# A two-layer graph network on one core: load order, place of a weight set-up, the last output, and how norms get their reciprocal root

## The chip, the core and the metric

The kernel runs on one core of a Trainium2 chip. A core has a matrix engine (TensorE, PE), a vector engine (VectorE, DVE), an activation engine (ScalarE, ACT), a general engine (GpSimd, POOL) and a queue engine (SyncE, SP). Each works through its own instructions in order, and they wait for each other by semaphores. The metric is device time in microseconds (us) for one execution; lower is better. Times given are medians over runs, and the profile shows one execution of the program.

## The reference

128 graphs of 128 nodes with 256 features go through two layers. Layer 0 is an attention layer with 8 heads, whose values depend on the kind of edge; layer 1 is a graph attention applied twice. Each layer ends in two layer norms with a feed-forward network between them. Cut to what matters:

```python
def layer0(src, adj):                      # Wq, Wk, Wv[r], Wo, W1, W2, g1, beta1, ...
    q, k = heads(src @ Wq + bq), heads(src @ Wk + bk)
    attn = softmax(q @ k.T / sqrt(32))
    out = sum((attn * (adj == r)) @ heads(src @ Wv[r] + bv[r]) for r in range(4))
    x = ln(src + merge(out) @ Wo + bo, g1, beta1)
    return ln(x + gelu(x @ W1 + b1) @ W2 + b2, g2, beta2)

def gat(h, adj, W, a):
    Wh = h @ W
    e = leaky_relu(Wh @ a[:256] + (Wh @ a[256:]).T, 0.2)
    return softmax(where(adj > 0, e, -9e15), axis=1) @ Wh

def layer1(x, adj):
    h = ln(x + gat(gat(x, adj, W1, a1), adj, W2, a2), g_ln1, b_ln1)
    return ln(h + relu(h @ w_ff1 + b_ff1) @ w_ff2 + b_ff2, g_ln2, b_ln2)

def ln(x, g, b):
    return (x - mean(x)) / sqrt(var(x) + 1e-5) * g + b
```

## The kernel before

The fast pass handles the graphs in 32 groups of G = 4 (512 tokens, T). A slower general pass follows, which a flag computed at the end switches on only for inputs that the fast pass can't treat; with these inputs it does not run. All arithmetic is in 32-bit floats.

**A group's way.** `layer0` makes `qT` and `kT` (L382, L386) and the values `v` of the four graphs (L392, L396), then for each of two pairs of graphs `scores` (L319, with Exp on ACT, L326, and the masked copy `pm` on DVE, L327) and `attended` (row sums `pden` at L342, products `pav` at L352, reciprocal and scaling on DVE), then the product with Wo (`pwo`, L412). `norm0` normalises, `x1T` transposes on PE, `first_ffn` is the network with Gelu, `layer1` holds the norm, the folded graph attention (`pw`, `pb`, `py`, `pg`) and its edge weights (`edges`, with a second use of Exp at L427). `norm2`, `x3T`, `second_ffn` (with Relu) and `written` end the group.

**What overlaps.** PE's order is written out by hand (`manual_schedule`), and the order on the other engines is found by the framework's scheduler. While PE runs `first_ffn` of group g, the units of `layer0` of group g+1 are put between its matmuls (`beside`); beside `second_ffn` of group g-1 go the units of `layer1` of group g. The first group's `layer0` runs alone ahead of the loop. The network's inner tiles `ph` and `po`, like `pq`, `pv`, `pwo` and the set-up's tiles, come from one PSUM pool, `ps_mm`, with two buffers (tag `mm`). ACT empties each `ph` into `hT` (L284), and PE can start the next but one only then.

**Norms.** `normed` (L231) takes statistics on DVE for each graph (L237, L238), adds EPS on DVE (L240), raises to the power -0.5 on GpSimd (L241, with the constant tile `mhalf`) and scales on DVE (L243). `scaled` multiplies and adds the norm's weights on GpSimd (L250, L251). There are four norms per group.

**The start.** Loads are issued from SP (`w`, `load`) and from ACT (`col`, `row`) in program order: Wq, Wk, then xT, adj and x of the first group, Wv, Wo, the networks' weights, and last the two graph weights and their vectors a1, a2, into a temporary tile that shares a buffer with `hT`. The set-up of the graph layer (L191 to L219) makes products of weights and vectors on DVE (`columns`, L89), transposes the first graph weight on PE (`pgt`), multiplies it by the second (`pgw`) and copies the results to `wu` and `wb`. It comes ahead of the first group's matmuls in PE's order. A check of each adj (L373) runs on DVE as the group is entered.

**The end.** `written` (L497) normalises a group, scales it on GpSimd, and writes all four graphs with one DMA of 512 KB.

Of the kernel before, what the change touches and what calls it, by code (L numbers as in the profile page):

```python
# [10 lines left out]
F32 = mybir.dt.float32  # L11
I32 = mybir.dt.int32
AF = mybir.ActivationFunctionType
ALU = mybir.AluOpType
# [3 lines left out]
EPS = 1e-5  # L18
# [6 lines left out]
P = 128  # L25
G = 4
T = G * P
# [3 lines left out]
class Weights:  # L31
# [40 lines left out]
    def constants(self):  # L72
        nc = self.nc
        self.ident = self.tile([P, P], "ident")
        make_identity(nc, self.ident)
        self.ones = self.tile([P, P // 4], "ones")
        nc.vector.memset(self.ones, 1.0)
        self.eps = self.tile([P, 1], "eps")
        nc.vector.memset(self.eps, EPS)
        self.mhalf = self.tile([P, G], "mhalf")  # L80
        nc.vector.memset(self.mhalf, -0.5)

    def columns(self, wt, arow, scr, name):

# [15 lines left out]
def flat(t):  # L100
    return t.rearrange("p b d -> p (b d)")


def fast_pass(ctx, tc, a, out):
# [13 lines left out]
    NF = FF // P  # L118
# [10 lines left out]
    ps_mm = ctx.enter_context(tc.tile_pool(name="ps_mm", bufs=2, space=PSUM))  # L129
    k = Weights(tc, const, a)  # L130

    def load(g):
        xt = io.tile([P, NCH, T], F32, tag="xT", name=f"xT_{g}")
        nc.sync.dma_start(
            xt, xT[:, g * T : (g + 1) * T].rearrange("(c p) t -> p c t", p=P)
        )
        ad = w3p.tile([P, G, P], I32, tag="adj", name=f"adj_{g}")
        nc.sync.dma_start(ad, adjT[:, g * G : (g + 1) * G, :])
        xr = io.tile([P, G, D], F32, tag="x", name=f"x_{g}")
        nc.sync.dma_start(  # L140
            xr, x[g * T : (g + 1) * T, :].rearrange("(b p) d -> p b d", p=P)
        )
        return xt, ad, xr


    k.constants()
    wq, wk = k.w("L0_gnn_Wq"), k.w("L0_gnn_Wk")
    first = dict(zip(("xt", "ad", "xr"), load(0)), g=0)
    bq, bk = k.col("L0_gnn_bq"), k.col("L0_gnn_bk")

    wv = k.tile([P, NCH, 2, D], "wv")
    for c in range(NCH):
        nc.sync.dma_start(
            wv[:, c], a["L0_gnn_Wv"][0:2, c * P : (c + 1) * P, :].rearrange("r p n -> p r n")
        )
        nc.vector.tensor_sub(wv[:, c, 1], wv[:, c, 1], wv[:, c, 0])
    bv = k.row("L0_gnn_bv", 2 * D)
    nc.vector.tensor_sub(bv[:, D:], bv[:, D:], bv[:, :D])
    wo, bo = k.w("L0_gnn_Wo"), k.row("L0_gnn_bo")
    w1, b1 = k.w("L0_gnn_W1"), k.col("L0_gnn_b1")  # L160
    w2 = k.w("L0_gnn_W2")
    g1c, be1c = k.col("L0_gnn_g1"), k.col("L0_gnn_beta1")
    g2c, be2c = k.col("L0_gnn_g2"), k.col("L0_gnn_beta2")
    g1r = k.row("L0_gnn_g1")

    be1b2 = k.row_sum("L0_gnn_beta1", "L0_gnn_b2")
    g2r, be2r = k.row("L0_gnn_g2"), k.row("L0_gnn_beta2")
    u1, c1 = k.w("L1_gnn_w_ff1"), k.col("L1_gnn_b_ff1")
    u2 = k.w("L1_gnn_w_ff2")
# [8 lines left out]


    NU = D + 3  # L180

    temp = flat(w1p.tile([P, NF, T], F32, tag="hT", name="temp"))
    taken = [0]

    def cut(*shape):
        n = math.prod(shape)
        taken[0] += n
        t = temp[:, taken[0] - n : taken[0]]
        return t.rearrange("p (c n) -> p c n", c=shape[0]) if len(shape) > 1 else t

    gw1, gw2 = (k.w("L1_gnn_W" + s, cut(NCH, D)) for s in "12")  # L191
    a1, a2 = (k.row("L1_gnn_a" + s, t=cut(2 * D)) for s in "12")
    scr = cut(D)
    wa1 = k.columns(gw1, a1, scr, "1")
    wa2 = k.columns(gw2, a2, scr, "2")
    rhs = cut(NCH, D + 2)
    nc.vector.tensor_copy(rhs[:, :, :D], gw2)
    nc.vector.tensor_copy(rhs[:, :, D : D + 1], wa2[:, :, 1:2])
    nc.vector.tensor_copy(rhs[:, :, D + 1 : D + 2], wa2[:, :, 0:1])
    gw1T = cut(NCH, D)  # L200
    for m in range(NCH):
        pt = mm_tile(f"pgt_{m}")
        for c in range(NCH):
            nc.tensor.transpose(
                pt[:, c * P : (c + 1) * P], gw1[:, c, m * P : (m + 1) * P], k.ident
            )
        nc.scalar.copy(gw1T[:, m, :], pt[:, :D])
    wu = k.tile([P, NCH, NU], "wu")
    wb = k.tile([P, NCH, P], "wb")
    for m in range(NCH):  # L210
        pu = mm_tile(f"pgw_{m}")
        for c in range(NCH):
            nc.tensor.matmul(
                pu[:, : D + 2], gw1T[:, c, m * P : (m + 1) * P], rhs[:, c, :],
                start=(c == 0), stop=(c == NCH - 1),
            )
        nc.scalar.copy(wu[:, m, : D + 2], pu[:, : D + 2])
        nc.vector.tensor_copy(wu[:, m, D + 2 :], wa1[:, m, 1:2])
        nc.vector.tensor_copy(wb[:, m, :], wa1[:, m, 0:1].to_broadcast([P, P]))  # L219

# [5 lines left out]
    c_out = k.tile([P, NG, G, 2], "c_out")  # L226
# [4 lines left out]
    def normed(t, n, mv=None):  # L231

        st = small.tile([P, G, 6], F32, tag="st", name="st_" + n)
        if mv is None:
            mv = small.tile([P, G, 2], F32, tag="mv", name="mv_" + n)
        for b in range(G):
            nc.vector.bn_stats(st[:, b, :], t[:, b, :])  # L237
            nc.vector.bn_aggr(mv[:, b, :], st[:, b, :])  # L238
        rs = small.tile([P, G], F32, tag="rs", name="rs_" + n)
        nc.vector.tensor_scalar(rs, mv[:, :, 1], EPS, None, op0=ALU.add)  # L240
        nc.gpsimd.tensor_tensor(rs, rs, k.mhalf, op=ALU.pow)  # L241
        for b in range(G):
            nc.vector.tensor_scalar(  # L243
                t[:, b, :], t[:, b, :], mv[:, b, 0:1], rs[:, b : b + 1],
                op0=ALU.subtract, op1=ALU.mult,
            )

    def scaled(y, gr, br, n):
        o = w3p.tile([P, G, D], F32, tag="res", name="res_" + n)
        nc.gpsimd.tensor_mul(o, y, over(gr))  # L250
        nc.gpsimd.tensor_add(o, o, over(br))  # L251
        return o
# [47 lines left out]
    def beside(main, side):  # L300

        for units in side:
            for _ in range(units):
                next(main, None)
        for _ in main:
            pass
# [180 lines left out]
    def norm0(S):  # L487
        n = "0_%d" % S["g"]
        normed(S["t0"], n)
        S["res0"] = scaled(S["t0"], g1r, be1b2, n)  # L490

    def norm2(S):
        n = "2_%d" % S["g"]
        normed(S["t2"], n)
        S["res2"] = scaled(S["t2"], h1r, he1c2, n)

    def written(S):  # L497

        g = S["g"]
        normed(S["t3"], f"3_{g}", c_out[:, g])  # L500
        o = scaled(S["t3"], h2r, he2r, f"3_{g}")
        nc.sync.dma_start(
            out[g * T : (g + 1) * T, :].rearrange("(b p) d -> p b d", p=P), o
        )

    def first_ffn(S):
        S["t1"] = t = w3p.tile([P, G, D], F32, tag="t", name="t1_%d" % S["g"])
        return ffn(t, S["x1T"], w1, b1, AF.Gelu, w2, S["res0"], "0_%d" % S["g"])
# [6 lines left out]


    def entered(g):
        return dict(zip(("xt", "ad", "xr"), load(g)), g=g)

    def x1T(S):  # L520
        S["x1T"] = transposed(S["t0"], g1c, be1c, "0_%d" % S["g"])

    def x3T(S):
        S["x3T"] = transposed(S["t2"], h1c, he1c, "2_%d" % S["g"])
# [9 lines left out]

    with tc.manual_schedule(engines={mybir.EngineType.PE}):
        cur, prev = first, None
        for _ in layer0(cur):
            pass
        norm0(cur)
        x1T(cur)  # L540
        for g in range(NG):
            nxt = entered(g + 1) if g + 1 < NG else None
            if prev:
                norm2(prev)
            beside(first_ffn(cur), turn(nxt, prev))

            def after():
                if nxt:
                    x1T(nxt)

            side = layer1(cur, after)
            if nxt:
                first_units = next(side)
                norm0(nxt)
                side = itertools.chain([first_units], side)
            beside(second_ffn(prev) if prev else iter(()), side)
            if prev:
                written(prev)
            prev, cur = cur, nxt
        norm2(prev)  # L560
        x3T(prev)
        for _ in second_ffn(prev):
            pass
        written(prev)


    ok = k.tile([P, 5], "ok")
# [353 lines left out]
```

## Time and profile before

| | us |
|---|---|
| median of 3 runs | 3092.86 |
| lowest, highest | 3091.51, 3094.2 |
| the profiled execution, as timed | 3091.51 |
| its span in the trace, first to last instruction | 3089.7 |
| mean granted clock of TensorE | 0.992 of full speed |

| engine | busy, us | instructions |
|---|---|---|
| PE weight load (beside PE) | 2018.5 | 18062 |
| DVE | 1571.7 | 3434 |
| ACT | 989.0 | 1733 |
| POOL | 881.5 | 488 |

Some rows of the costliest groups that the change touches: the GpSimd power (L241) has 128 instructions of 1053 ns on average; the scaling after it (L243) 893 ns with the norm's own statistics and 384 instructions; the GpSimd multiplication of `scaled` (L250) 2357 to 2395 ns. In a line of these views the engine stands ahead of the operation, and what is written stands left of the arrow; the shape is partitions x elements; "x" and a number count instructions; the time in brackets is how long the engine had been idle, and what ended that. In the chain of waits each line is start, length and what it was, in order of time. PEld is PE's weight load, which runs beside its matmuls. The ends of matmuls are modelled, so they are good to some tenths of a microsecond.

### The profile page before, as it was taken

The numbers are of one execution on the slowest core, as the hardware profiler recorded it, in microseconds if no ns is written. First come the engines' busy times: TensorE is split into PE (matmuls) and PEld (weight loads), VectorE is DVE, ScalarE is ACT, GpSimd is POOL, SyncE is SP. The second block draws the span as 40 slices with busy tenths as digits, with TensorE's granted clock in tenths as the row PEclk, the third lists the DMA queues.
The fourth block names the chain that finished last, engine by engine and source line by source line (L and its number), as shares of the span: only waits on it lengthen the run. The fifth ranks groups of instructions, "written<-read, shape, count | busy, mean of one in ns | idle before, by whom it ended". The sixth has DMA issues, their size and how long they took to land.

```text
span 3089.7 us, 42733 instructions
## 1 busy us (share of the span) xinstructions
PE 2998.7 (97%) x18062; PEld 2018.5 (65%) x18062; DVE 1571.7 (51%) x3434; ACT 989.0 (32%) x1733; POOL 881.5 (29%) x488
## 2 busy tenths in 40 slices
PE   3989999999999999999999999999999999999996
PEld 2556676666676666676666676666676666676664
DVE  3444564554554554554554554554555554554523
ACT  1223333323333323333233333233333233333331
POOL 0213322313322313322323322323323223322222
PEclk9999999999999999999999999999999999999998
DMA  4000000000000000000000000000000000000000
GB/s 152 21 12 23 18 18 25 21 18 25 18 18 22 24 18 25 18 18 21 25 18 25 18 18 21 25 18 24 18 18 21 25 18 25 18 18 8 8 7 15
DMA packets 58101, 69.80 MB, mean 23 GB/s; under 512 B 6704, under 2 KB 44720, under 8 KB 57904
## 3 DMA queue, kind: packets, MB, share of 16 engines
q1 hardware_dynamic: 51632, 64.76, 6.9%
q8 instruction: 144, 2.36, 0.3%
q10 hardware_dynamic: 6272, 2.25, 0.3%
q14 instruction: 53, 0.43, 0.0%
HBM read 50.22 MB, written 16.78 MB: 22 GB/s over the span
## 4 chain that ended last, share of the span: by engine, by line
PE 94%; issue 3%; DMA 1%; DVE 1%; POOL 1%; ACT 0%; POOLq 0%; DVEq 0%; ACTq 0%
PE po L291 29%; PE ph L280 28%; PE pq L382 7%; PE pv L392 7%; PE pw L452 4%; PE pav L352 4%; PE pwo L412 3%; PE pt L260 3%; PE ps L319 2%; PE pden L342 2%; PE py L467 2%; PE pg L482 2%; PE pb L459 2%; PE pb L471 1%; DVE t L243 0%
## 5 line engine op out<-in xcount | busy, mean ns | idle before, releaser
L241 POOL TENSOR_TENSOR rs<-rs,mhalf 128x4 f32<-128x4 f32 x128 | 134.0, 1053 | 1610.6 <-DVE rs L240 1610.6
L280 PE MATMUL ph<-yT,w_L_gnn_W 128*128 128x512 f32 x1024 | 481.9, 594 | 0.0
L291 PE MATMUL po<-w_L_gnn_W,hT 128*128 128x256 f32 x2048 | 472.1, 384 | 0.0
L291 PE MATMUL po<-w_L_gnn_w_ff,hT 128*128 128x256 f32 x2048 | 457.5, 379 | 0.0
L280 PE MATMUL ph<-yT,w_L_gnn_w_ff 128*128 128x512 f32 x1024 | 456.5, 594 | 0.0
L291 PEld LDWEIGHTS po<-w_L_gnn_w_ff,hT 128*128 128x128 f32 x2048 | 386.5, 190 | 65.3 <-issue 14.8
L291 PEld LDWEIGHTS po<-w_L_gnn_W,hT 128*128 128x128 f32 x2048 | 381.4, 190 | 62.2 <-issue 6.6
L284 ACT ACTIVATE hT<-ph,c_L_gnn_b_ff 128x512 f32<-128x512 f32 x256 | 175.4, 685 | 684.6 <-PE ph L280 684.6
L243 DVE TENSOR_SCALAR t<-t,mv,rs 128x256 f32<-128x256 f32 x384 | 319.3, 893 | 126.2 <-POOL rs L241 126.2
L280 PEld LDWEIGHTS ph<-yT,w_L_gnn_W 128*128 128x128 f32 x1024 | 195.2, 191 | 245.5 <-issue 230.8
L396 DVE TENSOR_TENSOR v<-pv,r_L_gnn_bv 128x512 f32<-128x512 f32 x128 | 88.5, 691 | 484.4 <-PE pv L392 484.4
L280 PEld LDWEIGHTS ph<-yT,w_L_gnn_w_ff 128*128 128x128 f32 x1024 | 188.2, 191 | 205.4 <-issue 186.6
L284 ACT ACTIVATE hT<-ph,c_L_gnn_b 128x512 f32<-128x512 f32 x256 | 175.9, 687 | 441.3 <-PE ph L280 440.9
L392 PE MATMUL pv<-wv,xT 128*128 128x512 f32 x512 | 240.2, 592 | 0.0
L359 DVE RECIPROCAL rd<-pden 128x512 f32<-128x512 f32 x64 | 214.3, 3349 | 20.8 <-PE pden L342 20.7
L327 DVE TENSOR_TENSOR pm<-e,adj 128x512 f32<-128x512 f32 x256 | 159.5, 685 | 114.3 <-ACT e L326 114.3
L237 DVE BATCH_NORM_STATS2 st<-t 128x6 f32<-128x256 f32 x512 | 192.5, 413 | 5.5
L437 POOL TENSOR_TENSOR gs<-gs,gr 128x512 f32<-128x512 f32 x64 | 66.5, 1039 | 426.3 <-DVE gr L436 415.0
L326 ACT ACTIVATE e<-ps 128x512 f32<-128x512 f32 x256 | 132.1, 603 | 152.0 <-PE ps L319 151.7
L250 POOL TENSOR_TENSOR res<-t,r_L_gnn_g 128x1024 f32<-128x1024 f32 x64 | 150.8, 2357 | 87.2 <-DVE t L243 87.2
L392 PEld LDWEIGHTS pv<-wv,xT 128*128 128x128 f32 x512 | 94.9, 190 | 108.1 <-issue 108.1
L250 POOL TENSOR_TENSOR res<-t,r_L_gnn_g_ln 128x1024 f32<-128x1024 f32 x64 | 153.3, 2395 | 31.4 <-DVE t L243 31.4
(101 smaller groups left out, 3633.5 us busy)
## 6 DMA issues: line engine op xcount, KB each, us to landing
xT<-in_xT_dram SPq DMA_DIRECT2D x32, 512.0 KB, 3.7
x<-in_x_dram SPq DMA_DIRECT2D x32, 512.0 KB, 3.9
out_dram<-res SPq DMA_DIRECT2D x32, 512.0 KB, 2.9
adj<-in_adjT_dram SPq DMA_DIRECT2D x32, 256.0 KB, 2.7
w_L_gnn_W<-in_L_gnn_W_dram SPq DMA_DIRECT2D x2, 1024.0 KB, 9.1
w_L_gnn_w_ff<-in_L_gnn_w_ff_dram SPq DMA_DIRECT2D x2, 1024.0 KB, 9.5
wv<-in_L_gnn_Wv_dram SPq DMA_DIRECT2D x2, 256.0 KB, 7.8
temp<-in_L_gnn_a_dram ACTq DMA_DIRECT2D x2, 256.0 KB, 7.5
```

Source lines behind the costliest of these rows:

```text
L237: nc.vector.bn_stats(st[:, b, :], t[:, b, :])
L241: nc.gpsimd.tensor_tensor(rs, rs, k.mhalf, op=ALU.pow)
L243: nc.vector.tensor_scalar(t[:, b, :], t[:, b, :], mv[:, b, 0:1], rs[:, b : b + 1], op0=ALU.subtract, op1=ALU.mult,)
L250: nc.gpsimd.tensor_mul(o, y, over(gr))
L280: nc.tensor.matmul(ph, wa[:, c, f * P : (f + 1) * P], inT[:, c, :], start=(c == 0), stop=(c == NCH - 1),)
L284: nc.scalar.activation(hT[:, f, :], ph, func, bias=ba[:, f : f + 1])
L291: nc.tensor.matmul(po[:, s * D : (s + 1) * D], hT[:, f, b * P : (b + 1) * P], wb_[:, f, :], start=(f == 0), stop=(f == NF - 1),)
L326: nc.scalar.activation(e[:, s], pss[s], AF.Exp, scale=SCALE)
L327: nc.vector.tensor_mul(pm[:, s], e[:, s], ad[:, 2 * p : 2 * p + 2, None, :].to_broadcast([P, 2, NCH, P]),)
L359: nc.vector.reciprocal(rd, pden)
L382: nc.tensor.matmul(pq, w[:, c, m * P : (m + 1) * P], xt[:, c, :], start=(c == 0), stop=(c == NCH - 1),)
L392: nc.tensor.matmul(pv, xt[:, c, b * P : (b + 1) * P], wv[:, c].rearrange("p r d -> p (r d)"), start=(c == 0), stop=(c == NCH - 1),)
```

## The change

Four edits are made together.

1. The first group's xT is loaded ahead of the weights, adj and x behind Wv; the graph weights and a1, a2 come ahead of Wo and the networks' weights. Both queues, SP's and ACT's, get the new order.
2. The set-up of the graph layer becomes a generator, `graph_weights`, in two parts. The first (products on DVE, transposes) is taken up after the first scores of the first group, the second (the product of the weights) after the scores of its second pair.
3. The last group is written by `written_by_graph`: statistics, root, scaling and output graph by graph, with the norm's weights applied on DVE and four DMAs of 128 KB.
4. `normed` takes the square root on ACT and its reciprocal on DVE, in place of the addition on DVE and the power on GpSimd. `mhalf` is gone.

```diff
-    def load(g):
+    def load_xT(g):
         xt = io.tile([P, NCH, T], F32, tag="xT", name=f"xT_{g}")
...
+        return xt
+
+    def load_rest(g):
         ad = w3p.tile([P, G, P], I32, tag="adj", name=f"adj_{g}")
...
     k.constants()
+    first = {"g": 0}
+    first["xt"] = load_xT(0)
     wq, wk = k.w("L0_gnn_Wq"), k.w("L0_gnn_Wk")
-    first = dict(zip(("xt", "ad", "xr"), load(0)), g=0)
     bq, bk = k.col("L0_gnn_bq"), k.col("L0_gnn_bk")
...
+    bv = k.row("L0_gnn_bv", 2 * D)
+    first["ad"], first["xr"] = load_rest(0)
+    for c in range(NCH):
         nc.vector.tensor_sub(wv[:, c, 1], wv[:, c, 1], wv[:, c, 0])
...
+    gw1, gw2 = (k.w("L1_gnn_W" + s, cut(NCH, D)) for s in "12")
+    a1, a2 = (k.row("L1_gnn_a" + s, t=cut(2 * D)) for s in "12")
+    wo = k.w("L0_gnn_Wo")
+    g1c, be1c = k.col("L0_gnn_g1"), k.col("L0_gnn_beta1")
     w1, b1 = k.w("L0_gnn_W1"), k.col("L0_gnn_b1")
...
+    def graph_weights():
+
+        scr = cut(D)
+        wa1 = k.columns(gw1, a1, scr, "1")
+        wa2 = k.columns(gw2, a2, scr, "2")
...
+            nc.scalar.copy(gw1T[:, m, :], pt[:, :D])
+        yield
+        for m in range(NCH):
+            pu = mm_tile(f"pgw_{m}")
...
@@ normed
-        nc.vector.tensor_scalar(rs, mv[:, :, 1], EPS, None, op0=ALU.add)
-        nc.gpsimd.tensor_tensor(rs, rs, k.mhalf, op=ALU.pow)
+        sd = small.tile([P, G], F32, tag="sd", name="sd_" + n)
+        nc.scalar.activation(sd, mv[:, :, 1], AF.Sqrt, bias=k.eps)
         rs = small.tile([P, G], F32, tag="rs", name="rs_" + n)
+        nc.vector.reciprocal(rs, sd)
...
+    def written_by_graph(S):
+
+        g, t = S["g"], S["t3"]
+        o = w3p.tile([P, G, D], F32, tag="res", name=f"res_3_{g}")
+        for b in range(G):
...
+            nc.vector.bn_stats(st, t[:, b, :])
+            nc.vector.bn_aggr(mv, st)
+            sd = small.tile([P, 1], F32, tag="sd", name="sd_" + n)
+            nc.scalar.activation(sd, mv[:, 1:2], AF.Sqrt, bias=k.eps)
+            rs = small.tile([P, 1], F32, tag="rs", name="rs_" + n)
+            nc.vector.reciprocal(rs, sd)
+            nc.vector.tensor_scalar(
+                t[:, b, :], t[:, b, :], mv[:, 0:1], rs, op0=ALU.subtract, op1=ALU.mult
+            )
+            nc.vector.tensor_mul(o[:, b, :], t[:, b, :], h2r)
+            nc.vector.tensor_add(o[:, b, :], o[:, b, :], he2r)
+            r0 = g * T + b * P
+            nc.sync.dma_start(out[r0 : r0 + P, :], o[:, b, :])
...
-        for _ in layer0(cur):
-            pass
+        steps = graph_weights()
+        for i, _ in enumerate(layer0(cur)):
+
+            if i in (8, 9):
+                next(steps, None)
...
-        written(prev)
+        written_by_graph(prev)
```

More of the change, by code (lines that the diff above doesn't have):

```diff
@@ L79, in constants @@
         nc.vector.memset(self.eps, EPS)
-        self.mhalf = self.tile([P, G], "mhalf")
-        nc.vector.memset(self.mhalf, -0.5)
     def columns(self, wt, arow, scr, name):
@@ L142, in load @@
         )
-        return xt, ad, xr
+        return ad, xr
     k.constants()
+    first = {"g": 0}
+    first["xt"] = load_xT(0)
     wq, wk = k.w("L0_gnn_Wq"), k.w("L0_gnn_Wk")
-    first = dict(zip(("xt", "ad", "xr"), load(0)), g=0)
     bq, bk = k.col("L0_gnn_bq"), k.col("L0_gnn_bk")
@@ L155, in fast_pass, with cut @@
         )
+    bv = k.row("L0_gnn_bv", 2 * D)
+    first["ad"], first["xr"] = load_rest(0)
+    for c in range(NCH):
         nc.vector.tensor_sub(wv[:, c, 1], wv[:, c, 1], wv[:, c, 0])
-    bv = k.row("L0_gnn_bv", 2 * D)
     nc.vector.tensor_sub(bv[:, D:], bv[:, D:], bv[:, :D])
-    wo, bo = k.w("L0_gnn_Wo"), k.row("L0_gnn_bo")
+    bo = k.row("L0_gnn_bo")
+    temp = flat(w1p.tile([P, NF, T], F32, tag="hT", name="temp"))
+    taken = [0]
+    def cut(*shape):
+        n = math.prod(shape)
+        taken[0] += n
+        t = temp[:, taken[0] - n : taken[0]]
+        return t.rearrange("p (c n) -> p c n", c=shape[0]) if len(shape) > 1 else t
+    gw1, gw2 = (k.w("L1_gnn_W" + s, cut(NCH, D)) for s in "12")
+    a1, a2 = (k.row("L1_gnn_a" + s, t=cut(2 * D)) for s in "12")
+    wo = k.w("L0_gnn_Wo")
+    g1c, be1c = k.col("L0_gnn_g1"), k.col("L0_gnn_beta1")
     w1, b1 = k.w("L0_gnn_W1"), k.col("L0_gnn_b1")
-    w2 = k.w("L0_gnn_W2")
-    g1c, be1c = k.col("L0_gnn_g1"), k.col("L0_gnn_beta1")
-    g2c, be2c = k.col("L0_gnn_g2"), k.col("L0_gnn_beta2")
     g1r = k.row("L0_gnn_g1")
     be1b2 = k.row_sum("L0_gnn_beta1", "L0_gnn_b2")
+    w2 = k.w("L0_gnn_W2")
+    g2c, be2c = k.col("L0_gnn_g2"), k.col("L0_gnn_beta2")
     g2r, be2r = k.row("L0_gnn_g2"), k.row("L0_gnn_beta2")
@@ L180, in fast_pass @@
     NU = D + 3
[L182 to L207, printed above, removed]
@@ L208, in fast_pass @@
     wu = k.tile([P, NCH, NU], "wu")
     wb = k.tile([P, NCH, P], "wb")
[L210 to L219, printed above, removed]
+    def graph_weights():
+        scr = cut(D)
+        wa1 = k.columns(gw1, a1, scr, "1")
+        wa2 = k.columns(gw2, a2, scr, "2")
+        rhs = cut(NCH, D + 2)
+        nc.vector.tensor_copy(rhs[:, :, :D], gw2)
+        nc.vector.tensor_copy(rhs[:, :, D : D + 1], wa2[:, :, 1:2])
+        nc.vector.tensor_copy(rhs[:, :, D + 1 : D + 2], wa2[:, :, 0:1])
+        gw1T = cut(NCH, D)
+        for m in range(NCH):
+            pt = mm_tile(f"pgt_{m}")
+            for c in range(NCH):
+                nc.tensor.transpose(
+                    pt[:, c * P : (c + 1) * P], gw1[:, c, m * P : (m + 1) * P], k.ident
+                )
+            nc.scalar.copy(gw1T[:, m, :], pt[:, :D])
+        yield
+        for m in range(NCH):
+            pu = mm_tile(f"pgw_{m}")
+            for c in range(NCH):
+                nc.tensor.matmul(
+                    pu[:, : D + 2], gw1T[:, c, m * P : (m + 1) * P], rhs[:, c, :],
+                    start=(c == 0), stop=(c == NCH - 1),
+                )
+            nc.scalar.copy(wu[:, m, : D + 2], pu[:, : D + 2])
+            nc.vector.tensor_copy(wu[:, m, D + 2 :], wa1[:, m, 1:2])
+            nc.vector.tensor_copy(wb[:, m, :], wa1[:, m, 0:1].to_broadcast([P, P]))
@@ L504, in written @@
         )
+    def written_by_graph(S):
+        g, t = S["g"], S["t3"]
+        o = w3p.tile([P, G, D], F32, tag="res", name=f"res_3_{g}")
+        for b in range(G):
+            n = f"3_{g}_{b}"
+            st = small.tile([P, 6], F32, tag="st", name="st_" + n)
+            mv = c_out[:, g, b, :]
+            nc.vector.bn_stats(st, t[:, b, :])
[6 more added lines that the diff above has]
+                t[:, b, :], t[:, b, :], mv[:, 0:1], rs, op0=ALU.subtract, op1=ALU.mult
+            )
+            nc.vector.tensor_mul(o[:, b, :], t[:, b, :], h2r)
+            nc.vector.tensor_add(o[:, b, :], o[:, b, :], he2r)
+            r0 = g * T + b * P
+            nc.sync.dma_start(out[r0 : r0 + P, :], o[:, b, :])
     def first_ffn(S):
@@ L517, in entered @@
     def entered(g):
-        return dict(zip(("xt", "ad", "xr"), load(g)), g=g)
+        xt = load_xT(g)
+        ad, xr = load_rest(g)
+        return dict(xt=xt, ad=ad, xr=xr, g=g)
     def x1T(S):
```

## The prediction

> **What bounds the kernel now.** I read the page's part 1, then the waits of the matrix engine (PE), the windows of steady periods, the chain of waits over the first 90 us, and the timeline of ScalarE (ACT) at the places where the change puts something.
>
> ```profile
> PE 2998.7 (97%) x18062; PEld 2018.5 (65%) x18062; DVE 1571.7 (51%) x3434; ACT 989.0 (32%) x1733; POOL 881.5 (29%) x488
> ...
> PE pgt L204 <- DMA temp<-in_L_gnn_W_dram: 37.8, 1, 37.8
> ...
> 1853.60:1946.55 92.95, 92.95 (x566) 62.69 (x565) 49.10 (x107) 30.80 (x54) 27.47 (x16) 1.00 0.07 21
> ```
>
> PE is the bound: one period (one group of four graphs) is 92.95 us long and PE is busy for 92.95 of them, so any new PE wait inside the loop lengthens the run. ACT has 62 us free per period, but it works in order and PE waits for it at fixed places. Outside the loop PE waits 37.8 us at the start for loads. The start, from the chain of waits (first three lines) and the timeline:
>
> ```profile
> 17.67 8.21 DMA w_L_gnn_W<-in_L_gnn_W_dram
> 25.90 7.12 DMA temp<-in_L_gnn_a_dram
> 33.04 8.90 DMA x<-in_x_dram
> ...
> 26.75 1.28 ACT L207 ACT_TABLE_LOAD   x1 [26.75 <-DMA r_L_gnn_b_ln<-in_L_gnn_b_ln_dram]
> 31.99 0.60 SPq L138 DMA_DIRECT2D adj<-in_adjT_dram  x1
> 51.81 3.60 PE L382 MATMUL pq<-xT,w_L_gnn_Wk 128*128 128x512 f32 x8
> 64.02 2.50 DVE L327 TENSOR_TENSOR pm<-e,adj 128x512 f32<-128x512 f32 x4 [1.02 <-ACT e L326]
> ```
>
> Each DMA waits for the one eight before it (the first `adj` is issued at 4.65, when Wq, issued at 0.75, has landed after 3.9), and ACT computes nothing until its own 24 DMA issues are through, at 26.75. Then two places of a steady period, A and C, from ACT's timeline, each followed by PE's stretch from the chain of waits:
>
> ```profile
> 1105.82 0.69 ACT L386 ACTIVATE qT<-pq,c_L_gnn_bq 128x512 f32<-128x512 f32 x1 [11.20 <-PE pq L382]
> 1106.52 1.28 ACT L284 ACT_TABLE_LOAD   x1
> 1107.82 0.69 ACT L284 ACTIVATE hT<-ph,c_L_gnn_b 128x512 f32<-128x512 f32 x1
> ...
> 1109.21 1.72 PE ph L280 x4
> ...
> 1173.95 1.47 ACT L263 ACTIVATE yT<-pt,c_L_gnn_beta,c_L_gnn_g 128x512 f32<-128x512 f32 x2
> 1175.59 0.63 ACT L427 ACTIVATE gs<-gs 128x512 f32<-128x512 f32 x1 [0.17 <-DVE gs L426]
> 1176.12 0.67 ACT L284 ACTIVATE hT<-ph,c_L_gnn_b_ff 128x512 f32<-128x512 f32 x1
> ...
> 1173.69 5.15 PE ph L280 x12
> ```
>
> The PSUM tiles `mm` have two buffers, so a `ph` group may start only when ACT has emptied the tile two before. At A, `hT` is done at 1108.51 and the group at 1109.21 needs it: 0.70 us to spare. At C, `hT` is done at 1176.79; the third group of the stretch starts at 1173.69 + 2 x 1.717 = 1177.12: 0.33 us to spare.
>
> **What the Trainium skill says.** "ScalarE: Activation LUTs", section "Table sets: the hidden batching unit": sqrt, exp and gelu are in different sets, relu and identity in every one. The trace agrees: two loads per period, ahead of Gelu (L284) and Exp (L326), none ahead of Relu or Identity. Its section "What ACT_TABLE_LOAD costs" gives 1283 ns and a drain of 1380 ns. The trace shows 1283 ns each time, but the next activation 0.02 us behind (1107.80, 1107.82), so I take 1.30 us. "Trace Analysis", section "Matmuls", wants groups rotated over PSUM banks so that one is emptied under the next; here that works with the 0.70 and 0.33 above. "DMA: Bandwidth & Descriptors", section "Issuing engines are not separate DMA queues": loads issued from SP and ACT share 16 engines; the start agrees, at some 350 GB/s from 28 to 40 us whichever queue issued.
>
> **The change, part by part.**
>
> *Square root, in the loop.* Removed per norm: a DVE add of 0.17 (L240) and a GpSimd power of 1.02 (L241). Added: an ACT Sqrt of 128x4 and a DVE reciprocal of 128x4 (0.18, as L436). The trace has no such Sqrt; by the skill's price in the section just named (280 ns + 0.833 per element, neighbours overlapping by 93) one is 0.28 and two 0.47, an estimate. The table is the cost. In the changed program as built, ACT's order in each period is: qT, load, Sqrt, Sqrt, load, hT (A); Exp scores, load, Sqrt, Sqrt, Relu (B); gs, yT, load, Exp, hT (C). Five loads in place of two.
>
> A: qT ends 1106.51; load to 1107.80; two Sqrt from 1107.82 to 1108.29 (their inputs are ready at 1105.96); load to 1109.59; hT from 1109.61 to 1110.30; with 0.04 to PE, 1110.34 in place of 1109.21. PE stalls 1.13 us. It occurs for groups 2 to 30, where the next group's qT and two norms meet: 29 x 1.13 = +32.8. (In group 1 the only Sqrt lies ahead of qT and costs nothing.) If the two Sqrt take 0.35 or 0.6 it is 1.0 or 1.25: +29 to +36.
>
> C: yT ends 1175.42; load to 1176.70; Exp from 1176.72; hT starts 0.53 behind it as before, ends 1177.92; PE at 1177.96 in place of 1177.12: 0.84 us. Groups 1 to 30: +25.2 (bounds +22 to +28). In group 31 hT stands ahead of that load.
>
> B: nothing. The load lies in ACT's idle stretch. The second Sqrt waits for DVE's statistics, queued directly after the `pwo` add that can start at 1158.2: add 0.69, statistics 0.75, aggregate 0.30, so 1160.0; Sqrt to 1160.3; hT to 1161.0, needed at 1161.57. Cover 0.57; queued behind this Sqrt is the Relu that PE waits for.
>
> GpSimd loses its powers and DVE its adds, neither with PE behind it in the loop. The normalisations come at most 1.5 us later (L243 ended at 1114.1; its transposes start at 1117.80).
>
> *Start.* PE no longer waits for the graph weights; it has xT and Wq by some 8 us. Two gates follow. (1) ACT still issues 24 DMAs ahead of its first activation, and the third `pq` waits for it. The last waits for a column load that itself stands eight behind another; a1 and a2 (0.5 MB) are now ahead of it. I take the end at 25.5 (24 to 27): table 1.3, first qT 0.7, so the third `pq` at 27.5, not 51.81: -24.3. (2) DVE's order holds the check of the second group's adj (L373) between the second-last and the last v add, ahead of pm. That adj stands behind the same bytes as before and landed at 31.99 + 8.5 = 40.5. Then 0.69 + 0.69, and pm ends at 44.4 in place of 66.52: -22.1. The later gate, (2), decides.
>
> The moved set-up costs little: DVE's twelve column and copy instructions (37.8 to 44.5 before) run at about 20 to 27, when a1, a2 and the two graph weights, now 7th and 8th on SP's queue, are there, ahead of the first v add near 31. Four transposes (1.09) fit in PE's wait for pm. Eight matmuls (3.78) stand ahead of the second `pden`, where PE waited 2.49 us and then for the second pm; 0.6 us may show, 2.4 if that cover fails. Wo, W1, W2, u1, u2 shift back on SP behind the graph weights; the first user of W1 comes at 68, and it is there near 30. On POOL, the third group's x add now precedes the first residual; that residual is used at 128.8 before, 36 us after it was ready. Start: -21.5 (-24 to -17, if the second adj comes at 38 or 45).
>
> *Exposed norms.* The norm before PE's first transposes, and those of the last two groups, sit on the chain: add, power and hand-overs, about 1.3, become Sqrt and reciprocal, about 0.5, with the table already in: -0.7, -0.8, -0.8 = -2.3 (0 to -3). In group 0 one Exp gets a load of 1.3, mostly given back by POOL being free earlier (it started gs at 159.50 after work ending at 158.57): +0.3 (-1 to +2).
>
> *Last output.*
>
> ```profile
> 3079.71 2.35 POOL res L250
> 3082.06 0.07 issue
> 3082.13 2.34 POOL res L251
> ...
> 3084.49 0.38 SPq L502 DMA_DIRECT2D out_dram<-res  x1
> ```
>
> The last add's statistics end at 3076.82 either way. Then two Sqrt (0.47), two reciprocals (0.3), a flag reduction in DVE's order (0.41), two scalings (0.75), four 128x256 two-tensor operations at 0.37 (half of L362's pair, 0.74): last DMA at 3080.3, not 3084.49, and 128 KB in place of 512: -4.5 (-3.5 to -5.5). Its first two graphs go out under PE's last matmuls.
>
> *Sum.* +32.8 + 25.2 - 21.5 - 2.3 + 0.3 - 4.5 = +30.0 (bounds +17 to +46). The profiled execution took 3091.51 (span 3089.7 and 1.8 around it), so 3121.5; the median, 3092.86, lies 1.35 above it: 3122.9. I forecast 3122.
>
> **The rivals.**
> - Only one stall is real. The ends of matmuls are modelled, and the margins are tenths of a microsecond. A alone: 32.8 - 28.0 = +4.8, 3098; C alone: -2.8, 3090. For it: C rests on 0.33 us. Against: each new load alone is 1.30, over both margins. Chance 0.09.
> - Faster: both loads are hidden. PE's real need for the emptied tile would come later than drawn by over a microsecond, and the loop stays at 92.95. Then -28.0: 3065. It decides as soon as the stalls fall under 28.0/30 = 0.93 us a period, against 1.97 forecast. For it: ACT is busy only a third of the time. Against: the loads lie behind busy ACT instructions, not in its gaps. Chance 0.06.
> - B stalls too: the second Sqrt waits longer for DVE than drawn and holds the Relu. At 0.6 us in 30 periods: +18, 3140. For it: a cover of only 0.57. Chance 0.08.
> - The start gains nothing, because the loads land no earlier in sum: 3144. Against: PE's 37.8 us wait was for graph weights alone, while xT and Wq were there before 9 us. Chance 0.03.
>
> **How the numbers follow.** My forecast has 0.74. Its own range is 3109 to 3137; the range for 8 in 10 reaches to B's stall, 3103 to 3142. A measurement of this kernel tells about 0.2% (6 us) from no change. Slower: 0.74 + 0.08 + 0.03 and a little of the first rival, 0.86; within: 0.08; faster: 0.06.
>
> **What would show it.** In the changed profile: 162 table loads in place of 65; a PE wait for ACT of 1.1 us at the second `ph` of each period and of 0.8 us at its last `ph` of the second network; a period of about 94.9; the first `pq` before 10 us, pm ending near 44; the last DMA 4 us sooner after the last add. A period still at 92.95 makes the forecast wrong; so does a first pm after 50.

## The result, and the profile after

| | before | changed |
|---|---|---|
| median, us | 3092.7 (4 runs) | 3139.6 (4 runs) |
| lowest, highest | 3091.5, 3094.2 | 3138.2, 3143.6 |
| span of the profiled execution | 3089.7 | 3136.4 |
| one period of the loop, from the chain of waits | 92.945 | 95.475 |
| table loads of ScalarE | 65 | 162 |

The changed kernel is slower by a factor of 1.0153, 95% interval 1.0136 to 1.0171: 46.7 us in the profiled execution, where the prediction had 30.0, and the median lies just beyond the forecast case's own range of 3109 to 3137, inside the range for 8 in 10, 3103 to 3142.

The page's busy time by engine, then the row of PE's waits that has most time (time in all, times, longest), and one period in the windows view (length, then busy time and count for PE, PE's weight loads, DVE, ACT and POOL, then clock, DMA share and GB/s), all of the changed kernel:

```profile
PE 3012.8 (96%) x18062; PEld 2012.6 (64%) x18062; DVE 1642.5 (52%) x3444; ACT 1138.3 (36%) x1961; POOL 741.8 (24%) x358
```

```profile
PE ph L291 <- ACT hT L295: 60.1, 60, 1.1
```

```profile
1905.40:2000.88 95.48, 93.48 (x565) 62.60 (x565) 51.21 (x107) 35.41 (x62) 23.24 (x11) 1.00 0.07 20
```

The 60 waits of PE for `hT` are new. They are 2.0 us of a period, but the period is 2.53 longer, and PE is *busy* for 0.5 us more than before with the same matmuls. The chain of waits at place A shows where that is (start, length, what):

```profile
1105.55 1.28 ACT L250
...
1106.85 0.49 ACT sd L250 x2
...
1107.35 1.28 ACT L295
...
1108.64 0.70 ACT hT L295
...
1109.39 1.98 PE ph L291 x4
1111.37 1.72 PE pq L393 x4
```

Table, two roots, table, `hT`: as forecast. But the `ph` group that had waited takes 1.98 us and the next one the usual 1.72. So each stall has 0.26 us more behind it, called the restart of PE from here on. PE's weight load in the same place, of the kernel before and of the changed one:

```profile
1108.62 0.19 PEld L280 LDWEIGHTS ph<-yT,w_L_gnn_W 128*128 128x128 f32 x1 [0.24 <-ACT hT L284]
```

```profile
1109.38 0.30 PEld L291 LDWEIGHTS ph<-yT,w_L_gnn_W 128*128 128x128 f32 x2 [1.97 <-ACT hT L295]
```

Before, the first weights of the group are loaded 0.43 us ahead of its first matmul (at 1109.05 in PE's timeline), while PE still works on the group in front; behind the stall they are loaded together with it (1109.39). That fits a restart, but no run takes the 0.26 apart. Place C looks alike:

```profile
1175.86 1.28 ACT L438
...
1177.78 0.58 ACT hT L295
...
1178.41 1.98 PE ph L291 x4
```

The start, in the chain of waits of the changed kernel. The second group's adj is issued at 30.49 and holds VectorE until 39.53, then come its check, the last v (left out here), and pm:

```profile
30.49 9.04 DMA adj<-in_adjT_dram
...
39.55 0.70 DVE scr L384 x2
...
40.85 4.57 DVE pm L338 x4
```

To sum up the profiled executions, I take one landmark that both kernels have, the run of 40 `po` matmuls in each pass of the loop. It comes first at 255.47 before and at 231.73 after, the last two at 2950.87 and 3022.25 before and at 3000.48 and 3073.07 after. PE waits 30 times at place C and 30 times at place A, but the last wait at A, in the second to last stretch, costs nothing. PE's timeline there, of the changed kernel, then of the kernel before:

```profile
3018.86 1.98 PE L291 MATMUL ph<-yT,w_L_gnn_W 128*128 128x512 f32 x4 [1.14 <-ACT hT L295]
...
3023.29 1.98 PE L271 MATMUL pt<-ident,t 128*128 128x128 f32 x7 [2.08 <-DVE t L254]
```

```profile
2972.74 1.13 PE L260 MATMUL pt<-ident,t 128*128 128x128 f32 x6 [2.09 <-DVE t L243]
```

In both kernels PE has to wait there for the norm that VectorE makes, 2.08 us still after the stall, so that norm sets the length of the stretch. The stalls that count are 29 x (1.14 + 0.26) + 30 x (0.86 + 0.26) = 74.2; one C lies ahead of the first landmark and is taken out of the row of the start:

| part | forecast | measured |
|---|---|---|
| stalls at A and C | +58.0 | +74.2 |
| start to the first landmark | -21.9 | -24.9 |
| second to last stretch (71.38 before) | -0.8 | +1.2 |
| last stretch (67.45 before) | -5.3 | -4.1 |
| sum | +30.0 | +46.4 |

The 0.3 left to the measured 46.7 is the rounding of these terms.

### The profile page after: what moved, and what is told of

The parts are those of the page before. It is cut to its first block, busy times and chain, and to the rows that moved or that the text cites. A ratio compares the mean times of both kernels' runs of the same rounds, so it can differ in the third digit from the quotient of the medians.

```text
span 3136.4 us, 42856 instructions
## 1 busy us (share of the span) xinstructions
PE 3012.8 (96%) x18062; PEld 2012.6 (64%) x18062; DVE 1642.5 (52%) x3444; ACT 1138.3 (36%) x1961; POOL 741.8 (24%) x358
## 4 chain that ended last, share of the span: by engine, by line
PE 88%; ACT 9%; DVE 1%; DMA 1%; issue 0%; SPq 0%; POOL 0%; ACTq 0%; POOLq 0%; DVEq 0%
PE po L302 29%; PE ph L291 24%; PE pv L403 7%; PE pq L393 5%; PE pav L363 4%; PE pw L463 4%; PE pwo L423 4%; PE ps L330 2%; PE pt L271 2%; PE pden L353 2%; PE py L478 2%; PE pg L493 2%; PE pb L470 2%; ACT yT L274 1%; ACT L438 1%; ACT L250 1%
## 5 line engine op out<-in xcount | busy, mean ns | idle before, releaser
L291 PE MATMUL ph<-yT,w_L_gnn_w_ff 128*128 128x512 f32 x1024 | 464.5, 597 | 25.8 <-ACT hT L295 25.8
L254 DVE TENSOR_SCALAR t<-t,mv,rs 128x256 f32<-128x256 f32 x384 | 447.1, 1225 | 3.5
L250 ACT ACTIVATE sd<-mv,eps 128x4 f32<-128x4 f32 x96 | 28.1, 292 | 500.4 <-DVE mv L248 500.4
```

Source lines behind the costliest of these rows:

```text
L254: nc.vector.tensor_scalar(t[:, b, :], t[:, b, :], mv[:, b, 0:1], rs[:, b : b + 1], op0=ALU.subtract, op1=ALU.mult,)
L291: nc.tensor.matmul(ph, wa[:, c, f * P : (f + 1) * P], inT[:, c, :], start=(c == 0), stop=(c == NCH - 1),)
```

## The experiments

Diffs are against the changed kernel where nothing else is said. "Power kept" means `normed` as it was before, on GpSimd, with edits 1 to 3 in place.

### Which edit costs

`e1_pow_kept`:

```diff
-        sd = small.tile([P, G], F32, tag="sd", name="sd_" + n)
-        nc.scalar.activation(sd, mv[:, :, 1], AF.Sqrt, bias=k.eps)
         rs = small.tile([P, G], F32, tag="rs", name="rs_" + n)
-        nc.vector.reciprocal(rs, sd)
+        nc.vector.tensor_scalar(rs, mv[:, :, 1], EPS, None, op0=ALU.add)
+        nc.gpsimd.tensor_tensor(rs, rs, k.mhalf, op=ALU.pow)
```

> The changed kernel with the norms' power kept on GpSimd (edits 1 to 3 alone). My theory: all of the loss is in edit 4. The profile of the changed kernel has 2.525 us more per period over 29 periods, 73.3 us in all, and about 1 us in the last group; without them 3139.6 becomes 3064 to 3067, some 27 us below the kernel before, with a period of 92.95 and two table loads per period. Rival 1 (part of the longer period comes from the moved loads, or from what they do to the loop): 3080 or more, period above 93.2.

Measured: 3067.1, ratio 0.9919 [0.9903, 0.9936]; the period is 92.94. One period in the windows view:

```profile
1978.30:2071.24 92.94, 92.94 (x566) 62.72 (x565) 49.13 (x107) 30.80 (x54) 27.45 (x16) 1.00 0.07 21
```

PE is busy for the whole period again. Of the 24.6 us by which this span (3065.1) is under that of before, 20.9 are gained ahead of the first landmark and 3.65 behind the last one. Rival 1 falls.

`e2_root_alone` is the kernel before with the opposite edit to this diff, edit 4, and no other.

> The kernel before with edit 4 alone (square root on ScalarE, reciprocal on VectorE). My theory: the two stalls come whole, 3092.7 + 73 + about 1 in the last group - 1.5 in exposed norms: 3163 to 3167, period 95.47, 162 table loads or one less. Rival 1 (the stalls need the moved loads too): 3120 to 3150.

Measured: 3166.8, ratio 1.0242 [1.0225, 1.0259], period 95.48. Edits 1 to 3 have no part in the stalls, and the two halves of the change add up: -25.7 (3067.1 against 3092.8) and +74.0 make +48.3, against 46.9 between the medians.

### Loads or instructions

`e3_no_table` leaves out the square root:

```diff
-        nc.scalar.activation(sd, mv[:, :, 1], AF.Sqrt, bias=k.eps)
+        nc.scalar.activation(sd, mv[:, :, 1], AF.Identity, bias=k.eps)
```

> The changed kernel with Identity in place of Sqrt in `normed`: the square root is left out, so the norms are scaled by 1/(var + eps); every instruction, hand-over and the reciprocal stays, but no table of its own is needed. My theory: the table loads alone stall PE. ScalarE's two small instructions at place A take 0.5 us, below the 0.70 that PE has to spare there, so the period is 92.95 and the time 3061 to 3066. Rival 2 (the instructions and hand-overs on ScalarE and VectorE cost, not only the loads): a period of 93.3 or more, 3075 or more.

Measured: 3064.3, ratio 0.9908 [0.9891, 0.9924], period 92.94, and no wait of PE for `hT` in the loop. ScalarE's timeline at place A of this kernel, from the end of qT at 1085.42 on:

```profile
1085.32 0.29 ACT L250 ACTIVATE sd<-c_out,eps 128x4 f32<-128x4 f32 x1
1085.50 0.28 ACT L250 ACTIVATE sd<-mv,eps 128x4 f32<-128x4 f32 x1
1085.81 1.28 ACT L295 ACT_TABLE_LOAD   x1
1087.10 0.69 ACT L295 ACTIVATE hT<-ph,c_L_gnn_b 128x512 f32<-128x512 f32 x1
```

The same instructions in the same order with one load fewer cost nothing: half a microsecond fits into PE's 0.70. Rival 2 falls; the whole cost in the loop is the table loads'.

### One place at a time

Places A and C belong to different norms: the roots at A are those of norms 2 and 3, and the Exp at C needs its table again only because of the roots of norms 0 and 1 at B. Both kernels have `mhalf` and choose per norm, the first with "23", the second with "01":

```diff
+        if n[0] in "23":
+            sd = small.tile([P, G], F32, tag="sd", name="sd_" + n)
+            nc.scalar.activation(sd, mv[:, :, 1], AF.Sqrt, bias=k.eps)
+            nc.vector.reciprocal(rs, sd)
+        else:
+            nc.vector.tensor_scalar(rs, mv[:, :, 1], EPS, None, op0=ALU.add)
+            nc.gpsimd.tensor_tensor(rs, rs, k.mhalf, op=ALU.pow)
```

> The changed kernel with the square root on ScalarE in the third and fourth norm of a group alone; the first two keep the power. My theory: only the stall at place A is left, 1.14 and a restart of PE of 0.26 per period: period 94.35, 3104 to 3108, four table loads per period. Rival 3 (the stalls share one cost: with one of them gone the other grows, or the restart is not a constant): a period of 95 or more, or of 94.1 and less.

> The changed kernel with the square root on ScalarE in the first two norms of a group alone; the other two keep the power. My theory: only the stall at place C is left, 0.86 and a restart of 0.26 per period: period 94.07, 3096 to 3100, four table loads per period. Rival 3 (the two stalls are not independent): a period of 94.4 or more, or of 93.8 and less.

Measured: 3108.0, ratio 1.0054 [1.0037, 1.0071], period 94.35; and 3100.7, ratio 1.0029 [1.0019, 1.0039], period 94.06 to 94.07 but for one. The periods are as expected; the second median lies 0.7 above its range. PE's waits, of the kernel with A alone and of the one with C alone:

```profile
PE ph L297 <- ACT hT L301: 34.3, 30, 1.1
```

```profile
PE ph L297 <- ACT hT L301: 26.1, 30, 1.1
```

1.14 and 0.87 us per wait, 30 of each. The periods exceed 92.94 by 1.41 and 1.13, so 0.27 and 0.26 come on top of the wait both times. Rival 3 falls: the two stalls are independent, and the restart is the same for both.

### Is the restart a constant

`e12_delay_four`, on edits 1 to 3 with the power kept, delays ScalarE at A without any new table:

```diff
                 nc.scalar.activation(S[o][:, m, :], pq, AF.Identity, bias=bias[:, m : m + 1])
+                if o == "qT" and m == 0 and g > 1:
+                    nc.scalar.activation(
+                        dm, S[o][:, m, None, :].to_broadcast([P, 4, T]), AF.Identity
+                    )
```

> Edits 1 to 3 with the power kept, and one more ScalarE instruction of 128x2048 (it copies qT four times over into a tile that nobody reads) right behind the qT of place A, from the third group on. It is an estimate from the trace's 0.69 for 128x512 that it takes 1.9 there. My theory (a stall is the delay less the 0.70 that PE has to spare, and each stall costs a restart of 0.26 whatever its length): period 92.94 + 1.9 - 0.70 + 0.26 = 94.4, some 3110. Rival 6 (the 0.26 is a share of the stall, or belongs to the table loads): the period is 94.1.

Measured: period 94.50, one execution of 3113.8. The chain of waits of this kernel at place A:

```profile
1103.34 1.91 ACT dm L402
...
1105.26 1.28 ACT L296
...
1107.30 1.98 PE ph L292 x4
```

A stall of 1.28 (the 30 waits sum to 38.6), again 1.98 behind it: 92.94 + 1.28 + 0.26 = 94.48. Rival 6 falls. A stall of this length has its restart whether a table load made it or another instruction.

`e13_delay_ten` has 10 in place of 4, Sqrt of zero times qT in place of Identity, and so a load of its own.

> The same with an instruction of 128x5120 and a table load of its own ahead of it: 4.4 + 1.3 = 5.7 of delay, a stall of about 5.0. My theory (constant restart): period 92.94 + 5.7 - 0.70 + 0.26 = 98.2, some 3226. Rival 7 (after an idle time of some 4 us and more PE runs its next matmuls at half speed for some us, as the starts show after idle times of 3.96 and 4.29 but not after 3.20): 1.7 to 3.5 more per period, 99.9 to 101.7, some 3280 to 3330.

Measured: one execution of 3301.8; the period alternates, for the most part between 100.04 and 101.3. The stall is 5.13, as worked out, so the constant restart gives 98.3; rival 7 is right. PE's timeline of this kernel, behind such a stall:

```profile
1273.78 3.78 PE L292 MATMUL ph<-yT,w_L_gnn_W 128*128 128x512 f32 x4 [5.13 <-ACT hT L296]
1277.36 3.12 PE L396 MATMUL pq<-xT,w_L_gnn_Wk 128*128 128x512 f32 x4
1280.31 1.88 PE L292 MATMUL ph<-yT,w_L_gnn_W 128*128 128x512 f32 x4
```

Four matmuls of 1.88 take 3.78 and then 3.12 before PE is at its pace again; the granted clock was 0.50 over the first four, 0.60 over the next. So the 0.26 holds for stalls of 0.87, 1.14 and 1.28, and not for one of 5.13.

### What holds the start

The prediction named two gates, ScalarE's DMA issues (1) and the check of the second group's adj on VectorE (2), and let (2) decide. In the changed kernel they turned out to lie close together, and three kernels on edits 1 to 3 with the power kept open one, the other, and both. `e9_check_late` takes the check from the head of `layer0` to its end:

```diff
             added(t, p, po, xr)
+        scr = w1p.tile([P, G, P], F32, tag="rd", name="scr_" + n)
+        nc.vector.scalar_tensor_tensor(
+            flat(scr), flat(ad), 1.0, flat(ad),
+            op0=ALU.subtract, op1=ALU.mult, accum_out=c_adj[:, g : g + 1],
+        )
```

`e10_vectors_late` takes the vector loads that only later stages need into the first group's units:

```diff
         for i, _ in enumerate(layer0(cur)):
+            if i == 3:
+                g1c, be1c = k.col("L0_gnn_g1"), k.col("L0_gnn_beta1")
+                b1, g1r = k.col("L0_gnn_b1"), k.row("L0_gnn_g1")
...
             if i in (8, 9):
```

> Edits 1 to 3 with the power kept, and the check of a group's adj moved behind the group's attention, so that VectorE no longer waits for the second group's adj ahead of the first pm. My theory: the two gates of the start lie 0.4 us apart (first e at 40.35, pm free to start at 40.77), so that opening this one alone gives 0 to 2 us against edits 1 to 3 alone. Rival 4 (this gate decides, as I had predicted; the other has room of some 17 us): 10 us or more.

> Edits 1 to 3 with the power kept, and 17 of the vector loads that ScalarE issues put later in the program, so that nine of them stand behind its first activations and ScalarE's first table load can come at about 14 in place of 23.9. The adj check stays ahead of pm. My theory: opening this gate alone gives 0 to 2 us against edits 1 to 3 alone, since VectorE then waits for adj until about 39.5. Rival 5 (ScalarE's issuing is the only gate): about 10 us.

> Both of the last two edits together, on edits 1 to 3 with the power kept. My theory: with both gates open the first pm ends about 10 us sooner and the time falls by 7 to 11 us against edits 1 to 3 alone, to 3054 to 3058, the fastest of all. Rival 4 or 5 (one gate alone decides): the same as the run that opens that gate.

| opened | median (lowest, highest) | against 3067.1 |
|---|---|---|
| gate 2, the check | 3068.3 (3067.2, 3070.3) | +1.1 |
| gate 1, ScalarE's issues | 3064.9 (3063.4, 3065.4) | -2.2 |
| both | 3057.6 (3055.0, 3062.8) | -9.6 |

The 3067.1 is from another chip, on which the kernel before took 3092.8, against 3091.8 on the chip of these three; held against the kernel before on its own chip each time, the differences are +2.1, -1.3 and -8.6. Neither gate alone holds the start; both together are worth more than four times the better one. Rivals 4 and 5 fall. With gate 2 alone open, VectorE waited for the first `e` of ScalarE instead, and the first pm began at 42.98, against 42.01 with neither open. In the trace of the kernel with both, the first pm ends at 37.2, against 46.7 with neither. That trace is of its slowest execution, 3062.8, so it does not show how the other three came to their 3055 to 3058. In the run with gate 1 alone, VectorE had done the first pm at 34.4 and then waited until 41.60 for adj, because the check now stood in front of the reciprocal behind pm.

`e14_pool_issues` gives all those vector loads to GpSimd's queue (`col` and `row` now issue from `k.vq`), with the check late as well:

```diff
     a1, a2 = (k.row("L1_gnn_a" + s, t=cut(2 * D)) for s in "12")
+    k.vq = nc.gpsimd
```

> Edits 1 to 3 with the power kept, the adj check moved behind the attention, and all vector loads from the third norm weights on issued by GpSimd, which has little to do at the start, so that ScalarE has six DMAs left and its first table load comes at about 6. My theory (ScalarE's issuing still held the first qT until 15.3 and the second kT until 25 in the run with both edits): the first pm ends near 26 in place of 37, and the time is 3044 to 3054. Rival 8 (the weights' own arrival sets the start from there on, or GpSimd's issuing holds the addition to x that the first norm needs): 3056 or more.

Measured: 3060.6 (3059.7 to 3061.8), ratio 0.9896 [0.988, 0.9913]. The first table load came at 5.85 and the last kT at 16.04, but the first pm ended at 38.3: my forecast for this run failed. Rival 8 has the time, and the reason in part: it is the arrival of weights, but by way of VectorE's order. VectorE's timeline of this kernel:

```profile
27.96 1.28 DVE L405 TENSOR_TENSOR v<-pv,r_L_gnn_bv 128x512 f32<-128x512 f32 x2
32.33 0.69 DVE L405 TENSOR_TENSOR v<-pv,r_L_gnn_bv 128x512 f32<-128x512 f32 x1 [3.08 <-PE pv L401]
```

A third gate was behind the other two: the set-up's products, which wait for the graph weights until 20.9 and end at 28.0, stand ahead of the first v in VectorE's order. PE, with two `mm` tiles, waited 7.76 us for that v.

`e15_idle_filled` goes on from there: the graph weights load ahead of the first adj and x, and the second part of the set-up moves into PE's idle stretch ahead of the first transposes (the second of these two edits):

```diff
-            if i in (8, 9):
-                next(steps, None)
+            if i == 8:
+                next(steps)
+        next(steps, None)
```

> The run with GpSimd's issues, and two edits more: the two graph weights load ahead of the first adj and x, so that VectorE's products for the set-up, which held the first v addition until 27.96 there, can begin some 4 us sooner than 20.9; and the product of the graph weights (pgw, 2.0 us on PE) moves from the second scores into PE's idle stretch ahead of the first transposes, which was 4.31 us long. My theory: PE's idle stretch falls below the 3.20 after which no slow matmuls were seen, so the first pq after it takes 1.9 in place of 3.6 and the transposes 1.65 in place of 2.2: 2.3 us; with 2 to 4 from the sooner products the time is 3054 to 3057, the first landmark of the loop 4 to 6 us sooner than 228.69. Rival 9 (the half speed after an idle stretch is not set by the idle stretch ahead of it): pq at 3.4 or more as before, and 3057 to 3060.

Measured: 3052.5 (3051.4 to 3053.8), ratio 0.9874 [0.9857, 0.989], first landmark at 221.81, period 92.94. It is the fastest of all, 39 us under the kernel before on the same chip (3091.5), and faster than expected. Part of the reason I gave was wrong. The products began at 20.11, only 0.8 sooner, but this time the first took 0.42 and not 2.85, with no addition to x on GpSimd beside it, and they were through at 24.3; the first pm ended at 33.2 in place of 38.3. The idle stretch did fall, to 2.29, but the matmuls behind it were slow all the same (last section), as rival 9 has it. The expectation took 3.20 us of idle time to be harmless from the changed kernel alone; in three kernels run before it (`e2_root_alone`, `e3_no_table`, `e5_root_norms01`) slow matmuls follow an idle time of just 3.20.

## Why the prediction was right in direction and 17 us short

**Place A, "PE stalls 1.13 us", 29 x 1.13.** The stall is 1.14, and the order and each duration at A came out as worked out: load 1.28, two roots in 0.49. What the sum lacked is the restart of 0.26 behind each stall. The count of 29 is right for what the stalls cost: PE waits a 30th time, for group 31, but waits for a norm there anyway.

**Place C, 0.84, 30 times.** 0.86, 30 times, again with 0.26 behind it. The restart at both places is 59 x 0.26 = 15.3 us, nearly all of the 16.7 that were missing; the sum had put it at nothing. The other errors (start -3.0, second to last stretch +2.0, last stretch +1.2, the stalls' own sizes +0.9) happen to cancel but for 1.1. The experiments with one place each (periods 94.35 and 94.06) and with a delay of another kind (94.50) show it apart from the tables. In the trace of before it could not be read off, since PE had no wait in the loop: all its groups there have their weights loaded ahead. The stalls themselves came within 0.02 us of the forecast, which took 1.30 for a switch of tables: at A and C the next activation begins 0.01 to 0.02 us behind the load of 1.28.

**Place B, nothing.** Right: both roots were done ahead of `hT`, and PE shows no wait there. The rival that lets B stall ended near the measured time (3140), by another mechanism; the 60 waits belong to A and C alone.

**Start, -21.5, "the later gate, (2), decides".** First pm: 45.4, forecast 44.4. ACT free at 23.91 (forecast 25.5), the third pq at 25.94 (27.5), adj landed at 39.53 (40.5), all close. Two sizes were off inside. PE's matmuls at the start took 5.68 and 5.91 for eight in place of 3.6 (the granted clock was 0.62 over the second eight), which took 2.3 us of gate 1's room: the first e began at 39.84, and pm, held by gate 2, at 40.77. So (2) decided by less than a microsecond, and opening it alone gained nothing (+1.1). And pm took 4.66 in place of 2.50, with the addition to x on GpSimd beside it.

**Exposed norms, -2.3.** The first norm saved 0.76 of PE's idle time, as forecast (3.96 before, 3.20 after). The transposes and first pq behind that idle time took 2.21 and 3.41 before, and 1.65 and 1.88 after, 2.1 us less, which is most of the 3 us by which the start beat its forecast. That was luck of this execution: with the same 3.20 of idle time the kernel with edit 4 alone took 2.21 and 3.62 (last section). In the second to last stretch "with the table already in" was wrong: the load of 1.28 stands behind an `hT` there and the root waits for it. Measured from the landmark, PE's last wait for that norm ends at 22.81, not at 21.87, so the norm cost 0.94 in place of saving 0.8; the other 0.3 of the row lies behind that wait. The very last one saved 0.85 between `pg` and `pt`, as forecast.

**Last output, -4.5.** From PE's last `po` to the end: 14.61 before, 11.03 after, -3.6. The sequence and its times came as forecast, and the last DMA was issued 4.6 us sooner. What is missing lies behind it: from the end of that issue to the end of the program went 5.9 us and not 4.8. The smaller transfer did finish faster: from issue to landing went 1.7 us, against 3.1 before. So the loss lies behind the last landing, from where to the end went 4.5 us, against 2.1. What fills that time the runs do not show.

**The rivals.** "Both loads are hidden" falls with the stalls; so does "only one stall is real". Kernels with one stall do exist, at 3108 and 3101. "The start gains nothing" falls with -24.9.

## What to carry to other kernels

Price a new wait on PE as the wait and a restart: here 0.26 us for stalls of about 1 us, and 1.7 to 3 us more for one of 5 us, behind which the clock was at half; both are read from the length of the matmul groups behind the wait. A cheap function on ScalarE can cost what its table costs twice over, since the function after it needs its own table back, and that may be at a place far behind (C, because of B); count the loads in the built order and hold each against what PE has to spare there. Where several loads and queues gate one start, opening one shows nothing until the others are open too, so try them together before you call one harmless.

## What the runs showed of the hardware that was not expected

**TensorE at half its clock behind a stretch with little work.** In PE's timelines at the first transposes, of the kernel before, of the changed one, and of the fastest one:

```profile
84.32 2.21 PE L260 MATMUL pt<-ident,t 128*128 128x128 f32 x8 [3.96 <-DVE t L243]
86.32 3.41 PE L382 MATMUL pq<-xT,w_L_gnn_Wq 128*128 128x512 f32 x4
```

```profile
62.35 1.65 PE L271 MATMUL pt<-ident,t 128*128 128x128 f32 x8 [3.20 <-DVE t L254]
63.83 1.88 PE L393 MATMUL pq<-xT,w_L_gnn_Wq 128*128 128x512 f32 x4
```

```profile
51.24 2.30 PE L274 MATMUL pt<-ident,t 128*128 128x128 f32 x8 [2.29 <-DVE t L257]
53.33 3.02 PE L391 MATMUL pq<-xT,w_L_gnn_Wq 128*128 128x512 f32 x4
```

In these traces the granted clock changes only at steps of 3.41 us and is either full or half. Cut at those steps, the time around these transposes is, in the same three kernels (PE's busy time is the second number behind the stretch, the clock the third from the end):

```profile
79.15:82.56 3.41, 1.21 (x6) 0.73 (x4) 3.24 (x12) 0.00 (x0) 0.00 (x0) 1.00 0.18 7
82.56:85.97 3.41, 1.65 (x7) 1.32 (x8) 1.45 (x5) 0.26 (x1) 1.77 (x2) 0.50 0.42 150
85.97:89.39 3.42, 3.42 (x7) 1.70 (x6) 0.00 (x0) 1.30 (x2) 3.42 (x2) 0.50 0.00 0
89.39:92.80 3.41, 3.41 (x9) 1.52 (x8) 0.00 (x0) 2.66 (x3) 2.79 (x2) 1.00 0.00 0
```

```profile
57.73:61.14 3.41, 1.42 (x7) 0.91 (x5) 3.21 (x11) 0.00 (x0) 0.00 (x0) 1.00 0.04 11
61.14:64.56 3.42, 2.21 (x10) 1.40 (x11) 1.63 (x6) 1.26 (x3) 0.66 (x1) 1.00 0.44 145
64.56:67.97 3.41, 3.41 (x9) 1.52 (x8) 0.00 (x0) 2.61 (x4) 3.41 (x2) 1.00 0.01 2
```

```profile
48.79:52.20 3.41, 1.11 (x4) 0.42 (x3) 2.17 (x10) 0.38 (x1) 1.04 (x1) 1.00 0.51 154
52.20:55.61 3.41, 3.41 (x9) 2.13 (x9) 0.00 (x0) 1.56 (x2) 3.38 (x2) 0.50 0.00 0
```

Half clock follows a stretch in which PE was busy for 1.21 or 1.11 us, not one with 1.42 or 2.21, and full clock comes back behind a stretch that was busy throughout. Over all 14 traces of this case, between the first change of clock and the last, the clock fell behind every stretch in which PE was busy for less than 0.41 of it and behind none with more than 0.56, and it rose again behind the first one with 0.86 or more. So what counts is not how long PE waits but how the wait falls on the steps: the 3.20 us of the changed kernel were split between two of them, the 2.29 of the fastest lay in one.

The Trainium skill, "TensorE: Matmul & The Clock Gate", section "What's actually happening", says that the array runs at half clock by default, that a busy window releases it and an idle one takes it back, and that the windows are free-running and 3413 ns long. The half clock and the steps of 3.41 us agree; an idle window, though, was here one in which PE still worked for up to about half of the time. Why the border lies between 0.41 and 0.56 and not at one value, these runs leave open.

**VectorE held by GpSimd.** The same four pm instructions took 2.50 us in the kernel before and 4.66 in the changed one, where GpSimd's addition to x ran from 41.08 to 43.68 beside them; with that addition elsewhere (the fastest kernel, from 42.02) pm took 2.50 again. The Trainium skill, "SBUF — State Buffer", section "Who interferes with whom", has the two engines share a pair of ports that one of them holds at a time; the 2.2 us that pm lost are close to the 2.60 of the addition.
